# Attention inside a four-layer kernel: other slots for the projection and output products, and rotations of queries that are held back some slots

## The chip, the cores and the metric

The kernel runs on one NeuronCore of a Trainium2 chip. A NeuronCore has several engines that each work through a queue of their own in order: TensorE (PE in the profile) multiplies matrices and transposes, VectorE (DVE), ScalarE (ACT) and GpSimd (POOL) do elementwise work, and SyncE (SP) issues most DMA transfers. Engines wait for each other by semaphores. The metric is the device time of one execution in microseconds (us); the number given for a kernel is the median of its runs.

## The reference

Four pairs of a conditioning layer and a feed-forward layer are added to `x` (64 sequences of 32 tokens, width 512), one after the other. The change lies in the third pair, in attention over a paged cache:

```python
q = einsum('bsd,ed->bse', x, Wq).reshape(b, s, 32, 128)   # Wk, Wv: 8 heads
q = rope(rmsnorm(q, q_norm_w), pos); k = rope(rmsnorm(k, k_norm_w), pos)
k_all = concatenate([k_cache[block_table], k]); v_all = concatenate([v_cache[block_table], v])
scores = where(valid, q @ k_all.T * SCALE, -1e30)         # 512 cached keys + 32 own keys
o = softmax(scores) @ v_all
return einsum('bse,de->bsd', o, Wo)
```

All matrices are float32. What counts below: queries and keys are projected, normalised and rotated before they are used, each sequence attends to 512 cached keys and its own 32, and the heads' outputs go through the output projection `Wo`.

## The kernel before

`emit` runs three stages: `layer0`, `layer1` and `attention`, with the rest (`Tail`) behind attention. Attention takes two thirds of the time, and the change is in it alone.

**Tiles and steps.** The 2048 tokens are 16 tiles of 128 tokens, four sequences in each. The 8 key heads are done in two halves of four. A *step* is one half of the heads with one tile; there are 32 steps. Two steps that follow each other are a *pair*; there are 16 pairs. A step has 16 *turns* (four sequences times four key heads), so a pair has 32 turns and the kernel 512. A turn handles 128 rows: four query heads times 32 tokens.

**A turn on TensorE.** The loop is at L1233. Turn `i` turns the probabilities of its own turn (`turned`, L1000: four transposes into `prT_ps`, copied by ScalarE at L1004), does the extra work of slot `2t`, makes the scores of the turn two ahead (`start(i + 2)`, `scores`, L974), does the extra work of slot `2t + 1`, and multiplies by the values (`values`, L1015, into the accumulators `po`). `scores` is followed on VectorE by an add of the mask that also takes the minimum (L991), on ScalarE by the exponential with its sum (L993), and on VectorE again by a reciprocal (L995) and a multiplication of the probabilities (L998). After each second sequence `own_part` (L1023) adds the sequences' own values and two copies (L1034, one on ScalarE, one on VectorE) empty `po` into `oT`. After each sequence four gathers on GpSimd's queue fetch the next values (L738), and VectorE copies own values into place (L745).

**The extra work.** Between the turns' own instructions the kernel places, by numbers of slots written out by hand, the projections of the pair that follows and the output projection of the pair before. A pair has 64 slots; a number from 64 on is a slot in the next pair. The order of TensorE's instructions is the program's: `on_pe` (L76) chains them. The other engines' queues are ordered by the framework's scheduler when the kernel is built.

Both projections use a scheme with seven products instead of eight for a 2 by 2 block matrix:

- `Projections.product` (L846): seven products `m` for each of three groups `g` of columns (`g = 0`: keys and values; `g = 1, 2`: queries), in the order 1, 2, 5, 6, 3, 7, 4. Each is four matmuls of 512 columns. ScalarE takes the result out for `m` 1 and 5 (L857), VectorE adds it for the others (L865); `m` 3 and 7 have a second add (L867, L870).
- After products 2, 3, 7 and 4 of the queries one block is complete, and its rotation (`rotated`, L768) is put on the list `soon`. The list is emptied at the start of the next slot (`the_rest`, called in `slot`, L1150). A rotation is a square on ScalarE (L761), on VectorE a sum (L763), a scaling (L764), two half-width products (L775) and one of full width (L778), and on GpSimd a power (L130), an add (L779) and a product (L780).
- `Projections.turned` (L874) transposes a rotated block on TensorE (`qkT_ps`), and ScalarE copies it to `qT` (L883), from which scores are made.
- `Outputs.product` (L936): seven products, each in two pieces `u = 0` and `u = 1` of eight matmuls of 256 columns. Both pieces go into one accumulator, taken out after the second (L955 on ScalarE or L959 on VectorE). Between the two pieces the accumulator stays in use.

All these products share the PSUM tag `mm` with two buffers:

```python
acc = ps.tile([P, D], F32, tag="mm", bufs=2, name="pq" if g else "pkv")     # L851
self.acc = ps.tile([P, D], F32, tag="mm", bufs=2, name="py")[:, :H]         # L941
```

Each product is followed by a request for the weights of the product four later (`next_wp`, `next_wo`: one transfer of 512 KB on SyncE's queue into one of four buffers). Requests stand on the list `later`, of which each slot issues up to two, between the parts of the keys' loads.

Of the kernel before, what the change touches and what calls it, by code (L numbers as in the profile page):

```python
# [664 lines left out]
def attention(c, known, x_in, y_part, y_out, sums, tail):  # L665
# [18 lines left out]
    with ExitStack() as outer:  # L684
# [63 lines left out]

        soon = []

        def the_rest():
            for f in soon:
                f()
            del soon[:]
# [286 lines left out]
        per = SEQ * HKP  # L1041
# [34 lines left out]
        outputs = [Outputs(n) for n in range(len(steps) // 2)]  # L1076


        later, to_come = [], {}
        wos, wos_to_come = [], [partial(wo_piece, o.h, m, u) for o in outputs for m in ORDER  # L1080
                                for u in range(2)]

# [67 lines left out]
        def slot(fs):  # L1150
            now = later[:]
            del later[:]
            the_rest()
            for f in now[:2]:
                f()
            later[:] = now[2:]
            for f in fs:
                f()

        for s, (h, T) in enumerate(steps):  # L1160
# [6 lines left out]
            def at(i, *fs):  # L1167
                to_come.setdefault(s * 2 * per + i, []).extend(fs)
# [3 lines left out]
            if s % 2 == 0:  # L1172
# [7 lines left out]
                if not last_pair:  # L1180
                    p = projections[n + 1]
                    if n == 0:
                        ats = ((12, 14, 16, 17, 18, 20, 22), (24, 26, 28, 32, 33, 34, 38),
                               (40, 42, 44, 48, 49, 52, 56))
                        then = ((0, 0, 0, 21), (0, 1, 0, 29))
                        for i, f in zip((3, 5, 6, 7, 10), (partial(p.x, 0), partial(p.x, 1), p.x_sums,
                                                           partial(p.tables, "k"), partial(p.tables, "q"))):
                            at(i, f)
                    else:
                        ats = ((2, 6, 8, 12, 14, 17, 20), (22, 26, 28, 32, 34, 36, 40),  # L1190
                               (42, 44, 46, 49, 50, 54, 58))
                        then = ((0, 0, 0, 13), (0, 1, 0, 27))
                        at(3, partial(p.tables, "q"))
                    for *what, i in (*then, (1, 0, 0, 35), (1, 0, 1, 41), (1, 1, 1, 43), (1, 1, 0, 51),
                                     (2, 0, 0, 53), (2, 0, 1, 57), (2, 1, 1, 67), (2, 1, 0, 69)):
                        at(i, partial(p.turned, *what))
                    for g in range(GB):
                        for m, i in zip(p.ORDER, ats[g]):
                            at(i, partial(p.product, g, m), partial(later.append, next_wp))
                    if n + 2 < len(projections):  # L1200
                        then = projections[n + 2]
                        for i, f in zip((30, 40, 59, 61, 62), (then.load, partial(then.tables, "k"),
                                                               partial(then.x, 0), partial(then.x, 1),
                                                               then.x_sums)):
                            at(i, f)
                else:
                    for i, f in zip((4, 8, 12, 16, 20), tail.weights(xp, wk, op, wp_tile)):
                        at(i, f)
                    at(43, tail.scaled)
                    for m, i in enumerate((45, 48, 49, 61)):  # L1210
                        at(i, partial(tail.fold, ps, m))
                    at(52, outputs[n].first_blocks)
                    for i, where in enumerate((52, 54, 57, 59)):
                        at(where, partial(outputs[n].product, i), partial(later.append, next_wo))
                if n:
                    out = outputs[n - 1]
                    at(0, partial(out.first_sums, nc.gpsimd))
                    if out.h:
                        at(14, out.befores)
                    ats = (0, 1, 5, 9, 13, 16, 17, 21, 25, 29, 32, 33, 37, 41) if last_pair else \  # L1220
                        (0, 1, 4, 10, 16, 18, 24, 30, 33, 38, 48, 52, 56, 60)
                    for i, where in enumerate(ats):
                        at(where, partial(out.product, i), partial(later.append, next_wo))
                        if i in (5, 7):
                            for u in range(2):
                                at(where, partial(out.next_sum, 6 if i == 5 else 3, u))
                    at(47 if last_pair else 63, out.store)
                else:
                    for i in (40, 46, 52, 58):
                        at(i, next_wo)  # L1230
            for at in range(2 * per):
                slots[at].extend(to_come.pop(s * 2 * per + at, []))
            for t in range(per):  # L1233
                i = s * per + t
                _, _, b, g = of(i)
                prT = turned(i)
                if g == HKP - 1:
                    own_prTs = ([] if b % 2 == 0 else own_prTs) + [own_turned(b)]
                slot(slots[2 * t])
                start(i + 2)  # L1240
                if g == 1:

                    keys_of(i - 1 + 2 * HKP)
                slot(slots[2 * t + 1])
                values(b, g, prT)
                if b % 2 and g == HKP - 1:
                    own_part(b, own_prTs, oTs[s])
# [348 lines left out]
```

## Time and profile before

| what | value |
|---|---|
| median of 3 runs | 3628.14 us (3626.78 to 3630.88) |
| the profiled execution's own time | 3624.15 us |
| its span, first to last instruction | 3622.4 us |
| TensorE busy | 3529.3 us, 97% |
| VectorE, GpSimd, ScalarE busy | 2094.9, 1604.6, 1315.1 us |
| mean granted TensorE clock | 0.996 |
| one pair in the middle (1839.6 to 1986.3 us) | 146.7 us |
| DMA in that pair | 0.78 of the engines' time, 248 GB/s |

How to read it: matmuls are pipelined, and their recorded ends are modelled, so the busy share of TensorE says little about small stalls. Four transposes of one group start 0.109 us apart though each is recorded with 0.275 us; four matmuls of 512 columns start 0.429 us apart and are recorded with 0.592 us. A stall is therefore best read from start to start; the idle time that the profile states for it is 0.15 to 0.2 us shorter. "Idle before, releaser" names what ended a wait.

### The profile page before, as it was taken

The numbers are of one execution on the slowest core, as the hardware profiler recorded it, in microseconds if no ns is written. First come the engines' busy times: TensorE is split into PE (matmuls) and PEld (weight loads), VectorE is DVE, ScalarE is ACT, GpSimd is POOL, SyncE is SP. The second block draws the span as 40 slices with busy tenths as digits, with TensorE's granted clock in tenths as the row PEclk, the third lists the DMA queues.
The fourth block names the chain that finished last, engine by engine and source line by source line (L and its number), as shares of the span: only waits on it lengthen the run. The fifth ranks groups of instructions, "written<-read, shape, count | busy, mean of one in ns | idle before, by whom it ended". The sixth has DMA issues, their size and how long they took to land.

```text
span 3622.4 us, 61570 instructions
## 1 busy us (share of the span) xinstructions
PE 3529.3 (97%) x19328; PEld 2629.3 (73%) x19328; DVE 2094.9 (58%) x5268; ACT 1315.1 (36%) x3110; POOL 1604.6 (44%) x1607
## 2 busy tenths in 40 slices
PE   8999999999998999999999999999999999999999
PEld 3444788888866777777777777777777777778755
DVE  5443222222237777767777777777776777767433
ACT  1111111111114544444444444444444544445311
POOL 0112432222226645546456465555565645645232
PEclk9999999999999999999999999999999999999999
DMA  5003543333336777787777777778778778777631
GB/s 210 26 26 136 176 136 117 105 103 103 100 120 207 241 253 242 248 257 242 252 236 248 256 242 246 249 249 257 254 249 262 238 258 254 252 249 247 205 95 62
DMA packets 610341, 716.00 MB, mean 198 GB/s; under 512 B 61826, under 2 KB 469378, under 8 KB 610018
## 3 DMA queue, kind: packets, MB, share of 16 engines
q1 hardware_dynamic: 557538, 539.01, 47.6%
q0 software_dynamic: 50176, 168.86, 13.7%
q10 hardware_dynamic: 2304, 4.20, 0.3%
q8 instruction: 158, 2.59, 0.3%
q14 instruction: 165, 1.35, 0.1%
HBM read 669.88 MB, written 41.94 MB: 197 GB/s over the span
## 4 chain that ended last, share of the span: by engine, by line
PE 87%; DVE 7%; ACT 2%; DMA 2%; issue 2%; POOL 1%; SPq 0%; DVEq 0%; ACTq 0%; POOLq 0%
PE po L712 12%; PE sc L986 11%; PE gate_up L366 11%; PE py L712 10%; PE pq L712 8%; PE prT_ps L707 5%; PE pkv L712 5%; PE pz L366 5%; PE po L1362 3%; PE ph L126 3%; PE pd L251 3%; PE po L366 2%; PE qkT_ps L707 2%; PE py L206 1%; DVE swapped L775 1%
## 5 line engine op out<-in xcount | busy, mean ns | idle before, releaser
L738 POOL DMA_INDIRECT vt<-in_v_rows,v_rows x512 | 507.5, 991 | 436.5 <-PE po L712 315.2
L986 PE MATMUL sc<-kt,qT 128*128 128x288 f32 (+1 forms) x2048 | 556.7, 394 | 13.6 <-DVE low L991 9.0
L993 ACT ACTIVATE pr<-pr,low 128x544 f32<-128x544 f32 x512 | 383.3, 749 | 505.6 <-DVE low L991 397.5
L712 PEld LDWEIGHTS po<-prT,vt 128*128 128x128 f32 x4096 | 520.6, 192 | 50.5 <-ACT prT L1004 23.0
L712 PE MATMUL po<-prT,vt 128*128 128x128 f32 x4096 | 544.6, 276 | 6.9 <-ACT prT L1004 6.7
L986 PEld LDWEIGHTS sc<-kt,qT 128*128 128x128 f32 x2048 | 384.4, 190 | 221.2 <-issue 107.7
L991 DVE CUSTOM_DVE_ANT_0 pr<-sc,mask 128x544 f32<-128x544 f32 x512 | 368.1, 719 | 149.4 <-PE sc L986 111.7
L998 DVE TENSOR_SCALAR pr<-pr,low 128x512 f32<-128x512 f32 x512 | 345.2, 674 | 11.5
L1004 ACT COPY prT<-prT_ps 128x512 f32<-128x512 f32 x512 | 293.4, 573 | 90.3 <-PE prT_ps L707 38.0
L707 PE MATMUL prT_ps<-ident,pr 128*128 128x128 f32 x2048 | 311.7, 275 | 7.1 <-DVE pr L998 6.9
L779 POOL TENSOR_TENSOR projected<-projected,swapped 128x512 f32<-128x512 f32 x160 | 208.4, 1302 | 193.4 <-DVE projected L778 144.4
L712 PE MATMUL pq<-wp,x_sums 128*128 128x512 f32 x512 | 241.6, 595 | 12.9 <-DVE projected L865 12.9
L707 PEld LDWEIGHTS prT_ps<-ident,pr 128*128 128x128 f32 x2048 | 237.2, 142 | 17.8 <-issue 9.3
L712 PE MATMUL py<-wo,oT 128*128 128x256 f32 x1024 | 243.4, 381 | 0.0
L995 DVE RECIPROCAL low<-low 128x1 f32<-128x1 f32 x512 | 82.2, 161 | 252.1 <-ACT pr L993 231.1
L130 POOL TENSOR_TENSOR rs<-rs,minus_half 128x4 f32<-128x4 f32 x160 | 187.1, 1169 | 75.3 <-DVE rs L764 41.9
L712 PEld LDWEIGHTS py<-wo,oT 128*128 128x128 f32 x1024 | 188.8, 191 | 22.6 <-issue 0.3
L996 ACT ACTIVATE own_pr<-pr,low 128x32 f32<-128x32 f32 x512 | 165.0, 322 | 91.3 <-DVE low L995 58.1
L452 DVE TENSOR_TENSOR sg<-sg,gate_up 128x256 f32<-128x256 f32 (+1 forms) x88 | 37.0, 421 | 269.1 <-ACT sg L451 269.1
L712 PE MATMUL py<-wo,o_sum 128*128 128x256 f32 x768 | 182.9, 382 | 2.1 <-DVE o_sum L922 2.1
L761 ACT ACTIVATE squares<-projected 128x512 f32<-128x512 f32 x160 | 101.0, 631 | 226.8 <-DVE projected L865 128.4
L712 PE MATMUL pq<-wp,xT 128*128 128x512 f32 x384 | 182.3, 597 | 0.2 <-issue 0.2
(242 smaller groups left out, 5833.6 us busy)
## 6 DMA issues: line engine op xcount, KB each, us to landing
kt<-in_kT SPq DMA_DIRECT2D x2048, 64.0 KB
wp<-in_sums SPq DMA_DIRECT2D x192, 512.0 KB
wo<-out_sums SPq DMA_DIRECT2D x128, 512.0 KB
wp<-in_WqT SPq DMA_DIRECT2D x96, 512.0 KB
wo<-in_WoT SPq DMA_DIRECT2D x96, 512.0 KB
wp<-in_WkT SPq DMA_DIRECT2D x32, 512.0 KB
xt<-x SPq DMA_DIRECT2D x48, 256.0 KB
in_sums<-sums POOLq DMA_DIRECT2D x24, 512.0 KB, 5.1
```

Of the source, the lines that this page charges most:

```text
L130: self.nc.gpsimd.tensor_tensor(t, t, self.minus_half[:, :n], ALU.pow)
L366: c.on_pe(nc.tensor.matmul(out, lhsT, rhs, start=start, stop=stop))
L707: c.on_pe(nc.tensor.transpose(pt[:, m, :], piece, c.ident))
L712: c.on_pe(nc.tensor.matmul(out, lhsT, rhs, start=first and i == 0, stop=last and i == len(pairs) - 1))
L738: nc.gpsimd.indirect_dma_start(out=vts[b % 2][:, n, :], out_offset=None, in_=a["v_rows"], in_offset=bass.IndirectOffsetOnAxis(ap=rows[h][: ...
L779: nc.gpsimd.tensor_tensor(src, src, tmp, ALU.add)
L986: c.on_pe(nc.tensor.matmul(sc[:, lo + n * PSIZE:lo + m * PSIZE].rearrange("p (n k) -> p n k", k=PSIZE), q, kt[:, n:m, g, :], start=True, s ...
L991: nc.vector.tensor_tensor_reduce(pr[:, :NK], sc[:, lo:lo + NK], masks[h, b], -SCALE, 3.0e38, ALU.add, ALU.min, low[:, 0:1])
L993: nc.scalar.activation(pr[:, :NK], pr[:, :NK], AF.Exp, bias=low[:, 0:1], scale=-1.0, accum_out=low[:, 1:2])
L996: nc.scalar.activation(own_prs[b % 2][:, g * S:(g + 1) * S], pr[:, L:NK], AF.Copy, scale=low[:, 2:3])
L998: nc.vector.tensor_scalar(pr[:, :L], pr[:, :L], low[:, 2:3], None, ALU.mult)
L1004: last_prT.append(nc.scalar.copy(prT, pt).ins)
```

## The change

The products keep their order within their kind, and TensorE, VectorE, ScalarE, GpSimd and the DMA queues issue the same instructions as before. Other things are altered in the pairs after the first:

- Slots of the output product's pieces: 4, 10 become 6, 8; 16, 18 become 16, 17; 24, 30 become 24, 26; 33, 38 become 32, 33; 48, 52 become 48, 49. (0, 1 and 56, 60 stay. The last pair keeps its own list.) Slots 16, 32 and 48 follow the turn that ends with `own_part`.
- Slots of the projections' products, moved so that the number of products in each turn stays the same.
- In all pairs, after products 2, 3, 7 and 4 of the queries `put_off` takes the rotation from `soon` and files it under a slot 2, 0, 2 or 4 slots after the next one. `slot` gets what is filed ahead of its own list.
- In all pairs, slots of the queries' transposes (`turned`) move from 35, 41, 43, 51, 53, 57, 67, 69 to 37, 43, 51, 53, 57, 65, 67, 73.

```diff
+        WAIT = {2: 2, 3: 0, 7: 2, 4: 4}
+        def put_off(i, to):
+            to.setdefault(i, []).extend(soon)
+            del soon[:]
...
-                        ats = ((2, 6, 8, 12, 14, 17, 20), (22, 26, 28, 32, 34, 36, 40),
-                               (42, 44, 46, 49, 50, 54, 58))
+                        ats = ((2, 4, 10, 12, 14, 18, 20), (22, 28, 30, 34, 36, 38, 40),
+                               (42, 44, 46, 50, 52, 54, 58))
...
-                    for *what, i in (*then, (1, 0, 0, 35), (1, 0, 1, 41), (1, 1, 1, 43), (1, 1, 0, 51),
-                                     (2, 0, 0, 53), (2, 0, 1, 57), (2, 1, 1, 67), (2, 1, 0, 69)):
+                    for *what, i in (*then, (1, 0, 0, 37), (1, 0, 1, 43), (1, 1, 1, 51), (1, 1, 0, 53),
+                                     (2, 0, 0, 57), (2, 0, 1, 65), (2, 1, 1, 67), (2, 1, 0, 73)):
                         at(i, partial(p.turned, *what))
                     for g in range(GB):
                         for m, i in zip(p.ORDER, ats[g]):
                             at(i, partial(p.product, g, m), partial(later.append, next_wp))
+                            if g and m != 1 and m != 5 and m != 6:
+                                at(i, partial(put_off, s * 2 * per + i + 1 + WAIT[m], waiting))
...
-                        (0, 1, 4, 10, 16, 18, 24, 30, 33, 38, 48, 52, 56, 60)
+                        (0, 1, 6, 8, 16, 17, 24, 26, 32, 33, 48, 49, 56, 60)
...
-                slot(slots[2 * t])
+                slot(waiting.pop(2 * i, []) + slots[2 * t])
...
-                slot(slots[2 * t + 1])
+                slot(waiting.pop(2 * i + 1, []) + slots[2 * t + 1])
```

## The prediction

> **What bounds the kernel now.** I read the page's head and chain first: TensorE.
>
> ```profile
> span 3622.4 us, 61570 instructions
> PE 3529.3 (97%) x19328; PEld 2629.3 (73%) x19328; DVE 2094.9 (58%) x5268; ACT 1315.1 (36%) x3110; POOL 1604.6 (44%) x1607
> PE 87%; DVE 7%; ACT 2%; DMA 2%; issue 2%; POOL 1%; SPq 0%; DVEq 0%; ACTq 0%; POOLq 0%
> ```
>
> No matmul is removed, so only TensorE's stalls can be won. The view of waits, for TensorE from 1250 to 3290 us (pairs 1 to 14), has in each line what waited, for whom, us in total, times and the longest:
>
> ```profile
> PE pq L712 <- DVE projected L865: 12.9, 12, 1.3
> PE prT_ps L707 <- DVE pr L998: 6.0, 14, 0.4
> PE pkv L712 <- ACT y L955: 3.1, 13, 0.2
> PE sc L986 <- DVE low L991: 2.5, 12, 0.2
> PE po L712 <- ACT prT L1004: 2.1, 13, 0.2
> ```
>
> Five waits, about once a pair each: the same places in every pair. TensorE's timeline of pair 5 gives the places (start, length, and at the end the idle time with its releaser). Turn 3, slot 6:
>
> ```profile
> 1855.24 0.27 PE L707 MATMUL own_prT_ps<-ident,own_pr 128*128 128x128 f32 x1
> 1855.75 1.98 PE L712 MATMUL pkv<-wp,xT 128*128 128x512 f32 x4 [0.24 <-ACT y L955]
> ```
>
> Turns 20, 23 and 25 (slots 40, 46, 50):
>
> ```profile
> 1931.36 0.63 PE L707 MATMUL prT_ps<-ident,pr 128*128 128x128 f32 x4 [0.43 <-DVE pr L998]
> ...
> 1946.80 1.18 PE L986 MATMUL sc<-kt,qT 128*128 128x288 f32 x4 [0.21 <-DVE low L991]
> 1948.14 1.16 PE L712 MATMUL po<-prT,vt 128*128 128x128 f32 x8 [0.16 <-ACT prT L1004]
> ...
> 1956.06 0.60 PE L707 MATMUL prT_ps<-ident,pr 128*128 128x128 f32 x4
> 1957.92 1.98 PE L712 MATMUL pq<-wp,x_sums 128*128 128x512 f32 x4 [1.25 <-DVE projected L865]
> ```
>
> Stalls are larger than the idle time stated. Transposes start 0.109 us apart, so the product after 1956.06 could have begun at 1956.50 and began 1.42 later. Counted like this, start to start against each group's usual step, pairs 1 to 14 lose 53 us: turn 25 16.5, turn 23 11.8, turn 20 8.7, turn 3 6.6, turn 8 1.2, and 8.4 (0.6 a pair) in spots that belong to the turns themselves, mostly own part and what follows it.
>
> **The change part by part.** *Pieces beside each other.* Instructions stay the same; what moves is how long a piece holds one of the two `mm` buffers. Before, pieces at 48 and 52 hold one; products 6 and 3 of the last group at 49 and 50 share the other. The second must wait until VectorE has added the first (L865), which stands in VectorE's queue behind a reciprocal that waits for the exponential: the 1.42 us. After, the pieces stand at 48 and 49 and products at 50, 52, 54 have both buffers. Going through the built order for which buffer each product takes and where its eviction stands, only the products at 2 and 4 still share one in a row, with 2.7 us of TensorE's work between (scores 0.92, transposes 0.44, values 0.90, transposes 0.44) for a copy of 0.59. So turn 25 goes: −16.5. At slot 6 the buffer was that of pieces 0 and 1, whose copy the scheduler had put on ScalarE behind an exponential two turns later; now it stands a turn earlier, and slot 4's product takes the other buffer: −6.6. Turn 8's product at 17, on a shared buffer, goes to 18: −1.2.
>
> *Rotations held back.* A rotation costs VectorE 2.32 us (0.67 + 2 × 0.41 + 0.68 + 0.15); a turn's softmax 1.63 (0.72 + 0.08 + 0.16 + 0.67); an eviction 0.69, two for products 3 and 7; mask 0.49, key copy 0.22. A turn on TensorE is about 4.0 us (0.44 + 0.92 + 0.90 and a product of 1.73), 4.4 with a transposed block. I summed VectorE's queue from the scores for one turn to the next in the built order. Before: 6.05 against TensorE's 4.43 for turn 19, then 4.37 against 4.11: VectorE is late by 1.9, and the probabilities of turn 20 with it. For turn 23: 5.36 against 4.43; the minimum, thus exponential and next scores, come late. After, for turns 19 to 25: 3.72, 5.34, 3.81, 3.29, 4.95, 3.40, 4.31 against 3.99, 4.54, 3.99, 3.99, 4.43, 4.10, 4.55. The worst excess is 0.80, no longer two in a row. Following turn 20's chain: probabilities ready 3.8 us after its scores, transposes reached 5.3 after: 1.5 spare. For turns 21 and 22 1.4 and 1.1 remain. The old order treated alike gives a stall of 0.7 at turn 20 (0.59 is there) and, at turn 23, 0.55 at the values (0.32) and none at the scores (0.37): good to about 0.3. So turns 20 and 23 go: −20.5.
>
> *What it queues up.* The tightest place left is turn 24: values need `po` emptied, and VectorE's copy (L1034, 0.69) comes 0.3 to 0.4 us before TensorE arrives; the two pieces at 48 and 49 (3.46 us) are its cover, and any delay shows one for one. I charge 0.3 us a pair, the method's error: +4. At a pair's end the rotation at 63 puts a sum and a product ahead of that copy (5.67 against 4.55 for turn 1), but `po` is wanted 6.7 us after the scores and free after 4.5. Nothing.
>
> *Later transposes.* From rotation to transposes there are 6 slots or more in both versions, some 13.7 us, for 2.3 on VectorE, 3.5 on GpSimd (1.17 + 1.30 + 1.04) and a set of gathers ahead of it on GpSimd (5.2). The earliest user is slot 65's block: scores at slot 66's end need it, with values, transposes and a product (3.1 us) as cover for a copy of 0.58 that stands before the exponential on ScalarE. Nothing; uncovered it would cost up to 1 us a pair.
>
> *Weights.* SyncE's requests move with the products, among the keys' 64 KB loads. By the order on SyncE and what each must wait for, the shortest lead is 7 slots, before (slot 50) and after (slot 42), about 16 us, but 7, 8 and 8 now follow each other. By the packets' times, 512 KB loads of `in_sums` landed 3.1 to 8.9 us after issue. Hidden, for either sign.
>
> *First pair.* Its products stay; rotations move. It loses 17.6 us to stalls, some 8 of them from turn 18 on. Sums for turn 18 don't change (6.03), for turn 19 they fall (4.87 to 3.36), for turn 23 rise (4.26 to 5.51), for turns 28 and 29 go from 3.96 and 2.73 to 2.04 and 4.24. Between −5 and +5; I take 0.
>
> **A rule against it.** The rows: L998 has 674 ns on average on the page, but
>
> ```profile
> L998 DVE TENSOR_SCALAR pr<-pr,low x446: 470/487/3033, 1250.8 to 3289.3; 128x512 f32<-128x512 f32 x149
> ```
>
> (shortest/median/longest): some 128 of the 446 are over 60 ns longer than the median, mostly beside GpSimd's adds, products and gathers. The Trainium skill, "SBUF — State Buffer", section "Who interferes with whom", explains this: VectorE's copies and `tensor_scalar` in two-port modes and GpSimd share a port pair that one holds for a whole instruction while the other blocks. The change brings rotations to 37, 41, 45, 47. By the rows (0.67 holds the average loss) the sum is as above. By the rule at its harshest each of six turns' L998 waits out a GpSimd operation of about 1.2 us in place of the 0.19 it loses on average: 6.1 us a pair, of which about 1.1 is spare, so 5.0 of new stall against 3.2 won, +25 us over 14 pairs. I take the rows: before, the same four rotations stand in 35 to 45, equally dense.
>
> **Sum.** −16.5 − 6.6 − 1.2 − 20.5 + 4 ± 0 = −40.8, say −40. Span 3622.4 − 40 = 3582.4; the execution's own time was 1.75 above its span (3624.15), the runs' median 4.0 above that: 3588.
>
> **Rivals.**
> - *Half of it comes back* (VectorE waits more between minimum and exponential than the sums show, so stalls move to turns 20 to 26): 20 us or fewer are won, 3605 to 3620. For it: from turn 20 to 25 VectorE's work after the change is 25.1 us against 25.6 of TensorE's. Against: recorded durations overlap on VectorE (a full product of 0.67 is followed after 0.60), so true loads are smaller.
> - *Slower, by the port*: the mechanism above, place turns 20 to 25. It decides from 4.3 us of added blocking a pair (3.2 won, 1.1 spare), 0.7 a turn; at its full price 3653. For it: L764 has 141 to 1269 ns. Against: nothing in GpSimd's amount of work changes, and the old stretch already has these blocks.
> - *No change*: the buffers are not what held TensorE, and another wait ends at the same time. Against: at 1957.92 the releaser is the eviction itself, and there was nothing else to wait for.
>
> **How the numbers follow.** A difference of 0.2% (7 us) is about what can be told from none. Likeliest, 3588 with own range 3577 (all 45 and the first pair won) to 3604: 0.76. Half back: 0.11. No change: 0.03. Slower: 0.10. Range 3577 to 3620 leaves out the last two and little else. Faster 0.87, same 0.03, slower 0.10.
>
> **What would show it.** Right: TensorE's wait for L865 (12.9) and for L955 (3.1) gone, waits for L998 and L991 under 2 us in all from pair 1 to 14, a pair of about 143.8 us in place of 146.7. Wrong: `po` waiting for L1034 at turn 24, `sc` for `qT` at slot 66, a product for `wp` at 42 to 46, or L998's mean well over 674 ns.

## The result

| | before | after |
|---|---|---|
| median of 6 runs each | 3627.46 us (3622.56 to 3632.71) | 3601.36 us (3597.67 to 3603.64) |
| ratio | | 0.9926, 95% interval 0.9916 to 0.9936 |
| span of the profiled execution | 3622.4 us | 3601.9 us |
| mean granted TensorE clock in it | 0.996 | 0.993 |
| typical pair in the middle | 146.7 us | 143.8 us |
| mean of pairs 1 to 14 | 146.4 us | 143.9 us |

The changed kernel is 26 us faster. The forecast was 3588 (3577 to 3620), 40 us faster: the direction and the range held, the size did not.

The changed kernel has seven more lines there, so line numbers behind L748 move by 7: the scores are L993, the minimum L998, the exponential L1000, the scaled probabilities L1005, the copy of `prT` L1011, the copy out of `po` L1041, the evictions L872 and L962, the rotation's sum, scaling, half products and full product L770, L771, L782 and L785, GpSimd's add and product L786 and L787, the first sums L929 and L930.

The page's head and chain:

```profile
span 3601.9 us, 61460 instructions
PE 3526.7 (98%) x19328; PEld 2634.1 (73%) x19328; DVE 2154.5 (60%) x5268; ACT 1301.2 (36%) x3110; POOL 1598.8 (44%) x1607
PE 84%; DVE 8%; DMA 3%; issue 2%; POOL 1%; ACT 1%; SPq 1%; DVEq 0%; another core or an unknown queue 0%; ACTq 0%; POOLq 0%
```

TensorE's waits from 1264.0 to 3277.9 us, which are pairs 1 to 14 here:

```profile
PE prT_ps L707 <- DVE pr L1005: 0.8, 1, 0.8
PE po L712 <- ACT prT L1011: 0.2, 1, 0.2
```

Five waits of 27 us in all have become two of 1 us. The timeline of TensorE shows turns 23 to 25 of a pair in the middle, where 1.42 us were lost before turn 25's product alone:

```profile
1945.08 1.16 PE L712 MATMUL po<-prT,vt 128*128 128x128 f32 x8
1946.17 1.16 PE L712 MATMUL po<-own_prT,own_vt 64*128 64x128 f32 x16
1947.26 0.66 PE L707 MATMUL prT_ps<-ident,pr 128*128 128x128 f32 x4
1947.76 1.89 PE L712 MATMUL py<-wo,o_sum 128*128 128x256 f32 x8
1949.49 1.08 PE L993 MATMUL sc<-kt,qT 128*128 128x288 f32 x4
1950.40 1.46 PE L712 MATMUL py<-wo,o_sum 128*128 128x256 f32 x6
```

The two pieces stand on either side of the scores, and no idle time is recorded (a bracket would stand at a line's end). In the first line, turn 23, something is still lost that the idle column leaves out: the four scores before it begin at 1943.87 and take 0.92, so the values could start at 1944.79 and start 0.29 later.

Stalls counted from start to start, as in the prediction, by turn over pairs 1 to 14 (us; turns 8, 23 and 31 hold 0.8, 1.3 and 1.4 that belong to the turns themselves):

| kernel | turn 3 | 8 | 20 | 21 | 23 | 25 | 31 | others | sum | pairs 1 to 14 last |
|---|---|---|---|---|---|---|---|---|---|---|
| before | 6.6 | 2.0 | 8.7 | 0 | 13.1 | 16.5 | 1.4 | 5.0 | 53.1 | 2049.0 |
| after | 1.2 | 3.5 | 0 | 0 | 6.8 | 0 | 1.6 | 5.3 | 18.4 | 2014.4 |

The sum falls by 34.7 and the 14 pairs by 34.6: the stalls account for all that happened in these pairs. But the span fell by 20.5 only. The rest was given back outside:

| stretch of the profiled execution | before | after | difference |
|---|---|---|---|
| ahead of attention (its code is unchanged) | 1066.0 | 1075.0 | +9.0 |
| first pair | 138.3 | 139.6 | +1.3 |
| pairs 1 to 14 | 2049.0 | 2014.4 | −34.6 |
| last pair | 149.8 | 153.6 | +3.8 |
| loads and products ahead of pair 0, and all behind the last pair | 219.2 | 219.3 | 0.1 |

**Ahead of attention** TensorE waits in the same places as before, a little longer. The two lines of waits up to 1070 us that differ most, after and then before ("issue": it waited for nothing that the profile shows):

```profile
PE pz L366 <- issue: 6.4, 3, 3.3
PE low_ps L366 <- issue: 4.5, 2, 4.1
```

```profile
PE pz L366 <- issue: 4.7, 3, 2.0
...
PE low_ps L366 <- issue: 3.4, 2, 3.0
```

That is 2.8 us. The larger part is what follows such a wait. In a table of windows of TensorE's activity (busy time and instructions of each engine; the third figure from the end is the granted clock), after and before:

```profile
801.00:808.00 7.00, 6.20 (x15) 4.97 (x16) 0.00 (x0) 0.59 (x1) 0.00 (x0) 0.51 0.01 2
889.00:896.00 7.00, 5.07 (x13) 4.00 (x14) 1.29 (x2) 0.59 (x1) 0.00 (x0) 0.56 0.01 2
```

```profile
801.00:808.00 7.00, 7.00 (x36) 6.18 (x35) 0.82 (x2) 0.97 (x2) 0.96 (x1) 0.98 0.17 40
889.00:896.00 7.00, 7.00 (x38) 6.28 (x37) 1.43 (x5) 2.48 (x6) 0.81 (x1) 1.00 0.14 37
```

In the first window a wait of 3.31 us ends at 801.80, and TensorE does 15 matmuls where the kernel before does 36: it works at half its clock (0.51 against 0.98). The stretches at half clock ahead of attention add up to 27.3 us after and 13.7 before; half of the difference, 6.8, with the 2.8 of longer waits makes 9.6, against the 9.0 observed. The Trainium skill, "TensorE: Matmul & The Clock Gate", "Part 1: The HAM clock gate", says that the clock is set by a free-running window of 3413 ns: after about one idle window it is halved, and after one of work it is whole again. The lengths here agree: each measures 3.4, 6.8 or 10.2 us (but for the last, which the end of the execution cuts). If that is so, equal waits can cost differently, by where in a window they fall; the run "rotations only" below has 14 equal waits of which half are followed by half clock.

The time ahead of attention goes with these stretches in all profiles of this case, whichever kernel: 13.7 us at half clock go with 1064.4 to 1067.2 us (both kernels are among these), 17.1 with 1067.1 to 1068.6, 20.5 with 1069.4 and 1070.3, 23.9 with 1071.1 and 1071.7, 27.3 with 1075.0 and 1075.2. So these 9 us belong to the execution, not to the change, as far as the profiles show. (The three profiles of the changed kernel start attention at 1071.1 us on average, those of the kernel before at 1066.3; so few can't tell this from chance.) What lengthens the waits by "issue" stays open.

**The last pair.** VectorE's timeline at its start:

```profile
3280.22 0.69 DVE L1041 COPY oT<-po 128x512 f32<-128x512 f32 x1 [1.05 <-remote]
3280.94 8.62 DVE L745 COPY own_vt<-v 32x128 f32<-32x128 f32 x5
3289.59 0.72 DVE L998 CUSTOM_DVE_ANT_0 pr<-sc,mask 128x544 f32<-128x544 f32 x1
```

and GpSimd's:

```profile
3279.20 0.95 POOL L738 DMA_INDIRECT vt<-in_v_rows,v_rows  x1 [0.30 <-issue]
3280.17 1.04 POOL L130 TENSOR_TENSOR rs<-rs,minus_half 128x4 f32<-128x4 f32 x1
3281.21 1.26 POOL L786 TENSOR_TENSOR projected<-projected,swapped 128x512 f32<-128x512 f32 x1
3282.64 1.05 POOL L738 DMA_INDIRECT vt<-in_v_rows,v_rows  x1 [0.17 <-issue]
3283.72 1.05 POOL L787 TENSOR_TENSOR projected<-projected,rs 128x512 f32<-128x512 f32 x1
3284.72 2.34 POOL L929 TENSOR_TENSOR o_sum<-oT 128x1024 f32<-128x1024 f32 x1
3287.14 2.34 POOL L930 TENSOR_TENSOR oT<-oT 128x1024 f32<-128x1024 f32 x1
```

Five copies of 32 by 128 took 8.62 us; one of them takes 0.22 when nothing is beside it. They end at 3289.56, right behind GpSimd's last sum (3289.48). Behind them on VectorE stands the minimum of turn 1, and TensorE's scores wait for it:

```profile
3284.20 0.60 PE L707 MATMUL prT_ps<-ident,pr 128*128 128x128 f32 x4
3290.47 2.15 PE L993 MATMUL sc<-kt,qT 128*128 128x288 f32 x4 [5.67 <-DVE low L998]
```

5.8 us are lost, and 6.8 us at half clock follow. The experiments come back to this.

### The profile page after: what moved, and what is told of

Read it like the earlier page. It is cut to its first block, busy times and chain, and to the rows that moved or that the text cites. A ratio compares the mean times of both kernels' runs of the same rounds, so it can differ in the third digit from the quotient of the medians.

```text
span 3601.9 us, 61460 instructions
## 1 busy us (share of the span) xinstructions
PE 3526.7 (98%) x19328; PEld 2634.1 (73%) x19328; DVE 2154.5 (60%) x5268; ACT 1301.2 (36%) x3110; POOL 1598.8 (44%) x1607
## 3 DMA queue, kind: packets, MB, share of 16 engines
q0 software_dynamic: 50176, 168.86, 13.4%
## 4 chain that ended last, share of the span: by engine, by line
PE 84%; DVE 8%; DMA 3%; issue 2%; POOL 1%; ACT 1%; SPq 1%; DVEq 0%; another core or an unknown queue 0%; ACTq 0%; POOLq 0%
PE po L712 12%; PE gate_up L366 11%; PE py L712 11%; PE sc L993 10%; PE pq L712 7%; PE prT_ps L707 5%; PE pkv L712 5%; PE pz L366 5%; PE po L1371 3%; PE ph L126 3%; PE pd L251 3%; PE po L366 2%; PE qkT_ps L707 1%; PE py L206 1%; DVE pr L1005 1%
## 5 line engine op out<-in xcount | busy, mean ns | idle before, releaser
L1000 ACT ACTIVATE pr<-pr,low 128x544 f32<-128x544 f32 x512 | 383.3, 749 | 688.1 <-DVE low L998 556.3
L993 PE MATMUL sc<-kt,qT 128*128 128x288 f32 (+1 forms) x2048 | 557.2, 395 | 15.5 <-DVE low L998 12.6
L993 PEld LDWEIGHTS sc<-kt,qT 128*128 128x128 f32 x2048 | 386.2, 191 | 232.2 <-issue 129.3
L998 DVE CUSTOM_DVE_ANT_0 pr<-sc,mask 128x544 f32<-128x544 f32 x512 | 368.4, 719 | 142.9 <-PE sc L993 119.2
L786 POOL TENSOR_TENSOR projected<-projected,swapped 128x512 f32<-128x512 f32 x160 | 208.3, 1302 | 313.5 <-DVE projected L785 284.5
L1005 DVE TENSOR_SCALAR pr<-pr,low 128x512 f32<-128x512 f32 x512 | 318.4, 622 | 12.6
L1011 ACT COPY prT<-prT_ps 128x512 f32<-128x512 f32 x512 | 294.0, 574 | 75.3 <-PE sc L993 30.8
L745 DVE COPY own_vt<-v 32x128 f32<-32x128 f32 x512 | 164.1, 320 | 22.8 <-issue 4.0
```

The lines of the kernel that those rows point to most:

```text
L786: nc.gpsimd.tensor_tensor(src, src, tmp, ALU.add)
L993: c.on_pe(nc.tensor.matmul(sc[:, lo + n * PSIZE:lo + m * PSIZE].rearrange("p (n k) -> p n k", k=PSIZE), q, kt[:, n:m, g, :], start=True, s ...
L998: nc.vector.tensor_tensor_reduce(pr[:, :NK], sc[:, lo:lo + NK], masks[h, b], -SCALE, 3.0e38, ALU.add, ALU.min, low[:, 0:1])
L1000: nc.scalar.activation(pr[:, :NK], pr[:, :NK], AF.Exp, bias=low[:, 0:1], scale=-1.0, accum_out=low[:, 1:2])
L1005: nc.vector.tensor_scalar(pr[:, :L], pr[:, :L], low[:, 2:3], None, ALU.mult)
L1011: last_prT.append(nc.scalar.copy(prT, pt).ins)
```

## The experiments

Times of one group were taken on one chip, each beside runs of the kernel before there. They came in three groups, and in the first the kernel before itself took 3606.26 us (3596.31 to 3611.09, 21 runs), some 23 us less than in the other sessions. No profile of it was taken there, so where these 23 us lie stays open; ratios of that group may be off by up to 0.6% against the others, and its kernels are best compared with each other and by their stalls. The stalls by turn, in pairs 1 to 14, counted as above:

| kernel | turn 3 | 8 | 20 | 21 | 23 | 25 | 31 | others | sum | pairs 1 to 14 last |
|---|---|---|---|---|---|---|---|---|---|---|
| changed (`e0_after`) | 1.1 | 0.8 | 0 | 0 | 6.7 | 0 | 1.6 | 5.2 | 15.4 | 2011.4 |
| slots only | 0 | 0.8 | 0 | 2.9 | 1.3 | 0 | 18.7 | 6.6 | 30.3 | 2026.4 |
| rotations only | 0.9 | 0.8 | 0 | 2.9 | 3.3 | 45.3 | 1.4 | 5.0 | 59.6 | 2055.6 |
| one pair of pieces | 6.6 | 0.8 | 8.6 | 0 | 13.0 | 0 | 18.8 | 5.6 | 53.3 | 2049.4 |
| that and the last rotation | 26.4 | 1.3 | 8.7 | 0 | 13.4 | 0 | 1.6 | 5.6 | 56.9 | 2053.0 |
| hold the last block only | 4.5 | 3.4 | 0 | 3.0 | 1.3 | 13.9 | 1.6 | 6.6 | 34.4 | 2030.5 |
| before again (`b0_before`) | 6.5 | 1.8 | 8.7 | 0 | 12.9 | 17.8 | 1.4 | 5.2 | 54.4 | 2050.3 |
| before again (`b1_before`) | 6.6 | 1.8 | 8.7 | 0 | 13.2 | 18.5 | 1.4 | 5.0 | 55.1 | 2051.0 |
| changed again (`c0_after`) | 1.0 | 3.0 | 0 | 0 | 6.6 | 0 | 1.6 | 5.2 | 17.4 | 2013.5 |

### First group: the two halves of the change

The changed kernel, unedited, as the base:

> The changed kernel again, for comparison on this chip: 26 us faster than before (ratio 0.9926). In its profile pairs 1 to 14 lose 18 us to TensorE's stalls where before they lost 53, and the last pair stalls 5.8 us at its turn 1. If the 9 us that the first profile lost ahead of attention (layers 0 and 1, which the change does not touch) belong to that execution, attention's first product starts near 1066 us again; if they belong to the program, near 1075 us.

Measured: 3587.85 us (3584.07 to 3591.54), ratio 0.9954 (0.9939 to 0.9970). In its profile pairs 1 to 14 take 2011.4 us with stalls of 15.4, attention starts at 1066.5, and the last pair takes 145.9. The five copies at the last pair's start took:

```profile
3267.25 0.69 DVE L1041 COPY oT<-po 128x512 f32<-128x512 f32 x1
3267.98 2.87 DVE L745 COPY own_vt<-v 32x128 f32<-32x128 f32 x5
```

So what happens in pairs 1 to 14 is the program's; what happened ahead of attention and at the last pair's start is not in every execution.

Slots only (the change without the rotations' delay):

```diff
                             at(i, partial(p.product, g, m), partial(later.append, next_wp))
-                            if g and m != 1 and m != 5 and m != 6:
-                                at(i, partial(put_off, s * 2 * per + i + 1 + WAIT[m], waiting))
```

> The changed kernel without holding rotations back: each is issued in the slot after its product again; product slots and transposes as changed. Theory (buffers and rotations are two separate causes): the stalls of turns 25 and 3 go with the slots, 24 us, and those of turns 20 and 23 stay or grow, as rotations now stand at 29, 37, 39, 41; 15 to 24 us faster than before, ratio 0.993 to 0.996. Rival (VectorE's queue is the one cause, and the slots help only through it): under 7 us, ratio above 0.998.

Measured: 3599.22 us, ratio 0.9978 (0.9971 to 0.9986); 11.4 us slower than the changed kernel beside it, and 15.0 in pairs 1 to 14. The row "slots only" answers in a way that the prediction's split doesn't have: the stalls of turns 20 and 23, which I had given to the rotations, are gone with the slots alone (2.9 come up at turn 21), and a new one stands at turn 31. So the expected 15 to 24 us did not come, and of the theory only turns 25 and 3 held. TensorE's timeline there, and VectorE's:

```profile
1973.72 1.18 PE L993 MATMUL sc<-kt,qT 128*128 128x288 f32 x4 [0.54 <-DVE low L998]
1975.07 1.16 PE L712 MATMUL po<-prT,vt 128*128 128x128 f32 x8 [0.16 <-ACT prT L1011]
```

```profile
1966.01 0.69 DVE L872 TENSOR_TENSOR projected<-pq,projected 128x512 f32<-128x512 f32 x1 [0.30 <-PE pq L712]
1966.81 2.24 DVE L782 TENSOR_TENSOR swapped<-projected,q_sin 128x256 f32<-128x256 f32 x1
```

The rotation of the last block goes out at slot 59, straight behind its eviction; the first half product takes 2.24 us in place of 0.41, beside a gather and an add on GpSimd, and VectorE has not made up for it at turn 31.

Rotations only (the old slots, with the delays and the later transposes):

```diff
-                                     (2, 0, 0, 53), (2, 0, 1, 57), (2, 1, 1, 67), (2, 1, 0, 69)):
+                                     (2, 0, 0, 57), (2, 0, 1, 65), (2, 1, 1, 67), (2, 1, 0, 73)):
...
+                            if g and m != 1 and m != 5 and m != 6:
+                                at(i, partial(put_off, s * 2 * per + i + 1 + WAIT[m], waiting))
```

> The changed kernel with the old slots of products: only the rotations are held back and the transposes later. Theory (two separate causes, and the rotation at slot 63 causes the last pair's stall): turns 20 and 23 lose their stalls, 20 us, turn 25 keeps its 1.4 us a pair, and the last pair gains a stall of some 9 us with the clock's half speed after it: 8 to 15 us faster, ratio 0.996 to 0.998. Rival (rotations alone make the gain): 26 us, ratio 0.993.

Measured: 3625.78 us, ratio 1.0057 (1.0041 to 1.0074), 37.9 us slower than the changed kernel beside it, where a gain on the kernel before had been expected. Turns 3, 20 and 23 lose 4.2 us in place of 28.4 (turn 21 gains 2.9), so these stalls go here too; but turn 25, expected to stay, grows from 16.5 to 45.3. The stall expected at the last pair's start did not come: that pair takes 145.9 us. TensorE's waits in that run, turn 25 of one pair on TensorE, what VectorE did in front of the eviction, and what GpSimd did beside it:

```profile
PE pq L712 <- DVE projected L872: 27.8, 13, 2.1
```

```profile
1963.25 1.12 PE L712 MATMUL pq<-wp,x_sums 128*128 128x512 f32 x2 [2.14 <-DVE projected L872]
```

```profile
1959.36 1.41 DVE L745 COPY own_vt<-v 32x128 f32<-32x128 f32 x1
1960.80 0.72 DVE L998 CUSTOM_DVE_ANT_0 pr<-sc,mask 128x544 f32<-128x544 f32 x1
...
1962.44 0.16 DVE L1002 RECIPROCAL low<-low 128x1 f32<-128x1 f32 x1 [0.91 <-ACT pr L1000]
1962.52 0.67 DVE L872 TENSOR_TENSOR projected<-pq,projected 128x512 f32<-128x512 f32 x1
```

```profile
1959.63 1.04 POOL L787 TENSOR_TENSOR projected<-projected,rs 128x512 f32<-128x512 f32 x1
```

One copy of own values took 1.41 us in place of 0.22, and ends at 1960.77, with the product of the delayed rotation on GpSimd (1960.67). In the kernel before no rotation stood there, and the copy took 0.22. The minimum, the exponential, the reciprocal and the eviction behind it come 0.9 to 1.2 us later, and the stall grows from 1.42 to 2.31. In seven of the 14 pairs 3.4 us at half clock follow, though the recorded wait is 2.13 or 2.14 in all 14. Six of these take 147.6 or 147.7 us, where the pairs without take 146.0 (one 146.9): 1.7 more, half of 3.4; the seventh is pair 14, which is shorter in every kernel. The stall of 1.42 before has no half clock behind it in any pair.

Two things are to be read from the two halves together. At turn 3 this run has the old slots 4 and 10 and still no stall: the scheduler has put the copy of `y` (L962, 1860.36 in pair 5) ahead of the exponential (1861.30), behind which it stands in the kernel before. So the place of that copy in ScalarE's queue is the cause, and the new slots are not the only way to move it. And both halves contain the later transposes, while every run with the earlier ones (the kernel before, and two below) keeps the stalls of turns 20 and 23. The transposes that move from slot 35 to 37 put 0.44 us of TensorE's work between the scores for turn 20 and the transposes that wait there; the stall at turn 20 is 0.62 a pair. What the transposes do alone was not tried, so the share of slots, delays and transposes in these two turns stays open.

One pair of pieces (the kernel before, with only the pieces at 48 and 52 put next to each other, and two products out of their way):

```diff
-                               (42, 44, 46, 49, 50, 54, 58))
+                               (42, 44, 46, 50, 52, 54, 58))
...
-                        (0, 1, 4, 10, 16, 18, 24, 30, 33, 38, 48, 52, 56, 60)
+                        (0, 1, 4, 10, 16, 18, 24, 30, 33, 38, 48, 49, 56, 60)
```

> The kernel before with one thing changed: output pieces at 48 and 49 (before 48 and 52), and the last group's products 6, 3 at 50, 52 (before 49, 50). Theory (a held accumulator buffer is what stalls turn 25): the wait of pq for L865 goes, 1.42 us less in each of 13 pairs and 0.1 behind it, 16 us faster in all, ratio 0.9955. Rival (another wait ends at the same time): within 5 us, with a new wait at turns 25 or 26.

Measured: 3621.19 us, ratio 1.0043 (1.0028 to 1.0059). Turn 25's stall is gone whole, 16.5 to 0, as the held buffer says. And nothing is won: pairs 1 to 14 take 2049.4 us, as before, since turn 31 now loses 18.8 in place of 1.4: the same stall as in "slots only", in a kernel with the old slots. (By time it is 15 us slower than the kernel before on that chip; without a profile of that one there, where these lie stays open.) Two readings fit. VectorE used to gain 1.4 us on TensorE while that stood at turn 25, and no longer does; or the two products that moved a turn back put their additions a turn nearer to the last block's rotation. This run changes both and doesn't tell them apart.

### Second group: does holding the last rotation finish the job?

The kernel before, unedited, for a profile beside these:

> The kernel before, profiled where the others of this call are. Theory (its stalls are its own, the same everywhere): attention from its first product to its last near 2386 us, pairs near 146.7 us, and a difference in its total comes from ahead of attention. Rival (its stalls depend on who gets the port that VectorE and GpSimd share, and so on the execution): pairs of another length, 145.5 us or so, and the difference sits in them.

Measured: 3631.15 us, ratio 1.0007 (0.9999 to 1.0015) against the other runs of the same kernel; stalls by turn as in the first profile within 1.3 us.

One pair of pieces, and the last block's rotation held from 59 to 63, with its last transposes at 73 in place of 69 (all else as before):

```diff
+                            if n and g == 2 and m == 4:
+                                at(i, partial(put_off, s * 2 * per + 63, waiting))
```

> The kernel with pieces at 48 and 49 and products at 50, 52, and in addition the rotation of each pair's last block held back from slot 59 to 63 (its transposes from 69 to 73). Theory (the stall that went at turn 25 came back at turn 31, because the rotation at 59 made VectorE late there): turn 31's 1.1 us at the scores and 0.3 at the values go, pairs of about 145.1 us instead of 146.5, some 19 us faster than the version with the pieces alone. Rival (VectorE is late at turn 31 for another reason): pairs stay at 146.5.

Measured: 3639.83 us, ratio 1.0034 (1.0021 to 1.0047). Turn 31's stall is gone (18.8 to 1.6) and turn 3 has it (6.6 to 26.4). TensorE's waits (line numbers move by 5 here):

```profile
PE pkv L712 <- ACT y L960: 12.3, 13, 0.9
PE prT_ps L707 <- DVE pr L1003: 11.9, 20, 1.2
```

The first line is the wait for the output product's copy on ScalarE at slot 6, which the change removes through its slots 6 and 8. On ScalarE that copy stands behind the exponential; the rotation at 63 makes the minimum late, the exponential with it, and so the copy. In two pairs (at 2439.27 and 2735.57) half clock follows two waits that end 1.7 us apart, of 1.18 or 0.94 us and 0.94 us, neither of which reaches 1.25 us alone. The stall has moved from turn 25 to 31 to turn 3, and kept its size: 16.5, 18.8 (17.4 of it new), 26.4 (19.8 new).

The changed kernel with the delay for product 4 alone:

```diff
-                            if g and m != 1 and m != 5 and m != 6:
+                            if g and m == 4:
```

> The changed kernel with the rotation held back after product 4 alone; after products 2, 3, 7 it is issued in the next slot again. Theory (of the holds, that of the last block does the work): pairs near the 143.6 us of the full change, against 144.7 without any hold; within 4 us of the full change. Rival (holds after 2 and 7 are needed for turns 20 to 25): pairs of 144.3 us or more.

Measured: 3611.41 us, ratio 0.9955 (0.9942 to 0.9969). Turn 31 is free, but turn 25 loses 13.9 us, in another form than before: scores and values that wait for VectorE, not a product for a buffer. By the order of the program, the rotation of product 4 of the middle group, held to slot 45, now falls on that of product 2 of the last group, which is due at 45 as well; in the changed kernel the latter waits until 47. So the delays are one schedule and not separate gains; that this meeting makes the 13.9 us is argued from the order, not shown.

The changed kernel with the last pair's first sums on VectorE, to take GpSimd out of that place:

```diff
-                    at(0, partial(out.first_sums, nc.gpsimd))
+                    at(0, partial(out.first_sums, nc.vector if last_pair else nc.gpsimd))
```

> The changed kernel with the two sums at the start of the last pair's output product on VectorE instead of GpSimd (as the end of the kernel has them). Theory (in one execution GpSimd held the shared port through a rotation and these sums, VectorE's copies took 8.62 us and TensorE stood 5.8 us): the last pair takes 145 to 147 us whatever the execution; 0 to 8 us faster than the changed kernel, and less spread. Rival (the stall had another cause): the last pair can take 153 us here too.

Measured: 3592.96 us (3587.05 to 3594.48), ratio 0.9899 (0.9885 to 0.9913). The profile's last pair takes 151.4 us with a stall of 3.0 at its turn 1, so the expected 145 to 147 was missed; the reading that fits is that the sums now cost VectorE time of its own.

### Third group: the last pair

The changed kernel and the kernel before, unedited, on this chip:

> The changed kernel unedited, as the base for the two runs with the early last rotation. Theory (who gets the port is drawn anew by each execution): pairs 1 to 14 take 2011 to 2015 us again, and the last pair either 146 or 150 to 154. Rival (the stall at the last pair's start is fixed by the program): 153 to 154 again. The time against before: ratio 0.990 to 0.996.

> The kernel before, unedited, with a profile on the same chip as the changed kernel. By what the first two profiles show its pairs 1 to 14 take 2049 to 2051 us and its last pair 149 to 151; the ratio is 1.000 within 0.0015. If its time is again near 3606 us, as in the session of the first experiments, the theory (the difference lies ahead of attention) has pairs of 146.4 us and attention starting at 1050 us or earlier; the rival (the pairs themselves are faster there) has pairs of 145.5 us or less.

Measured: changed 3601.38 us (3597.93 to 3602.69), ratio 0.9920 (0.9906 to 0.9933), pairs 1 to 14 in 2013.5 and the last pair in 156.6, above the 150 to 154 expected; before 3633.38, ratio 1.0005 (0.9996 to 1.0014), 2051.0 and 152.2. The low time of the first session did not come again, so the two accounts of it stay untested.

In the changed kernel the five copies took 8.59 us again, with 5.8 lost on TensorE. Across the three profiles of it, what differs is the copy out of `po` in front of them. In pairs 2 to 14 (but for pair 9, where no gather is beside it) it starts 0.02 to 0.03 us ahead of a gather of GpSimd's. In the last pair of `e0_after` both start in the same hundredth (3267.25), the copy does not wait, and of the five own copies four take at most 0.27 us and one 1.86, and all are through before GpSimd's product and sums follow each other. In the other two, VectorE is idle for 1.05 us, which the profile puts down to an unknown releaser and which ends 0.07 us behind the gather; the copies then run into these. That the gather holds the port that the copy wants is argued from these times, not shown. In these three profiles an order of starts that 0.02 us decide goes with a stall of 5.8. A copy out of `po` that is late for another reason has the same behind it: in "hold the last block only" and in "that and the last rotation" it waits for TensorE by the profile, and an own copy of 4.12 or 4.13 us and stalls of 5.8 and 6.1 follow.

The last block's rotation, in the one pair ahead of the last, at slot 59 in place of 63, so that GpSimd's add and product are done before the sums:

```diff
-                                at(i, partial(put_off, s * 2 * per + i + 1 + WAIT[m], waiting))
+                                at(i, partial(put_off, s * 2 * per + i + 1 + (0 if m == 4 and g == 2 and n + 2 == len(projections) else WAIT[m]), waiting))
```

> Edit: in the one pair ahead of the last pair, the rotation after product 4 of the last group goes out at slot 59 (as before the change) in place of 63; all else is as after the change. Theory (GpSimd's adds and products of that held rotation, followed by its sums for the output product, keep VectorE from the port at the start of the last pair; this is what made the last pair 153.6 us in the first profile of the changed kernel): the last pair takes 145 to 148 us, no stall of the scores over 1 us there, and the time is 3 to 8 us below that of the unedited changed kernel on the same chip, if that kernel's last pair is again 150 us or more; where it is 146, no difference. Rival (the sums on GpSimd alone do it): last pair unchanged, at 150 us or more.

Measured: 3593.54 us (3584.73 to 3603.16), ratio 0.9892 (0.9877 to 0.9907). The own copies there (shortest, median, longest in ns), in this kernel and in the unedited one on the same chip:

```profile
L745 DVE COPY own_vt<-v x8: 216/220/334, 3278.2 to 3281.6; 32x128 f32<-32x128 f32 x8
```

```profile
L745 DVE COPY own_vt<-v x8: 207/228/4125, 3274.1 to 3283.1; 32x128 f32<-32x128 f32 x8
```

GpSimd's first sum in this kernel:

```profile
3283.32 2.36 POOL L929 TENSOR_TENSOR o_sum<-oT 128x1024 f32<-128x1024 f32 x1
```

No copy is held any more, and the stall at turn 1 is gone, although the sums are still on GpSimd. But the last copy ends at 3281.8, 1.5 us before the sums begin, so this run does not show what the sums would do to copies that met them. The 14 profiles of this case agree on the rotation's part. With it at 63 and the sums on GpSimd the longest of these copies took 1.85 or 1.86 us in two and 4.12 or 4.13 in four; with the rotation at 59 it took 0.34 at most in seven. With the rotation at 63 and the sums on VectorE (`e5_sums_on_vector`) it took 1.62, so the 4.1 us need both. The last pair of this profile takes 152.3 us all the same, against the 145 to 148 expected: at its turn 14 TensorE waits 3.6 us for a load of keys and 2.2 more by "issue", then works at half clock. The kernel before has the same wait there (3.7), and `e0_after` (3.8). In `after` and `c0_after`, which were held up at turn 1, its longest was 2.0 and 2.5: so a part of the 5.8 us would have been spent at turn 14 anyway.

Both together:

```diff
-                    at(0, partial(out.first_sums, nc.gpsimd))
+                    at(0, partial(out.first_sums, nc.vector if last_pair else nc.gpsimd))
```

(and the edit of the run before.)

> Edit: as the run with the last rotation at slot 59, and the first sums of the last pair's output product on VectorE in place of GpSimd. Theory (both loads on GpSimd share the blame): last pair 145 to 147 us, time 3 to 8 us below the unedited changed kernel on the same chip. Rival (the sums cost VectorE what the port cost it): last pair 150 us or more, no gain over the run with the early rotation alone.

Measured: 3591.34 us (3586.22 to 3597.82), ratio 0.9893 (0.9880 to 0.9907), last pair 149.5 us, pairs 1 to 14 2015.2. No gain over the early rotation alone. Both are 8 to 10 us below the changed kernel on that chip, so the early last rotation is the better version of this change, at a ratio of 0.989 to the kernel before (the sums on VectorE alone, at 0.990 in the second group, can't be told from it); a part of the 8 to 10 is a higher clock over the whole run (mean of the runs 0.995 against 0.994, by estimate some 4 us), to which the half clock that followed the stall belongs.

## Why the prediction was right in direction and too large

- *TensorE's stalls alone can be won.* Right: 34.7 us of stalls less, 34.6 us of time less in the same pairs. The signs named for it came too: the waits for the eviction and for the copy of `y` are gone, and those for VectorE's softmax are 0.8 us in all.
- *Turn 25, −16.5, a held buffer.* Right, and shown alone: with those two pieces next to each other, and two products out of their way, it is 0. What the step lacked is the next place: removed alone, 17.4 us come back at turn 31. This term came out by luck: the delays of the rotations, which I had booked elsewhere, keep the 17.4 from coming back.
- *Turn 3, −6.6.* 1.2 left, mostly one instance, so −5.4. The cause, a copy on ScalarE behind an exponential, was confirmed when it grew to 26.4 in the run that made the exponential late, and when it went to 0.9 in "rotations only", where the copy stands ahead of the exponential with the old slots.
- *Turn 8, −1.2.* Wrong by sign and small: +1.5 in the first profile, −1.2 in `e0_after`.
- *Turns 20 and 23, −20.5, by the rotations' delays.* The size was −15.0: turn 20 gone (−8.7), turn 23 from 13.1 to 6.8 (−6.3). The attribution failed: either half of the change takes away most of the 20.5 (2.9 us are left at turns 20 to 23 with the slots, 4.9 with the rotations, 5.5 with both), so the gain can't be booked to the delays. Both halves have the later transposes, and whether these do it was not tried. The step summed VectorE's queue for the old and the new kernel, and never for a kernel with one part only. What is left at turn 23 is of the same kind as what went. ScalarE's timeline there, and VectorE's, beside the values that start at 1945.08 in place of 1944.79:

```profile
1943.72 0.75 ACT L1000 ACTIVATE pr<-pr,low 128x544 f32<-128x544 f32 x1 [3.82 <-DVE low L998]
...
1944.46 0.56 ACT L1011 COPY prT<-prT_ps 128x512 f32<-128x512 f32 x1
```

```profile
1941.25 0.68 DVE L872 TENSOR_TENSOR projected<-pq,projected 128x512 f32<-128x512 f32 x1
1941.85 0.86 DVE L771 TENSOR_SCALAR rs<-rs 128x4 f32<-128x4 f32 x1
1942.63 0.41 DVE L782 TENSOR_TENSOR swapped<-projected,q_sin 128x256 f32<-128x256 f32 x1
1942.96 0.71 DVE L998 CUSTOM_DVE_ANT_0 pr<-sc,mask 128x544 f32<-128x544 f32 x1
```

  ScalarE stood idle for 3.82 us until the minimum was there; the copy of `prT`, whose transposes were done by 1942.2, is behind the exponential in its queue. The minimum is late by a rotation, of which the scaling of 128 by 4 elements took 0.86 us in place of 0.16, its median before. My sums had 4.95 against 4.43 here, and followed the probabilities, not the copy that is queued behind the next exponential.
- *Turn 24's charge, +4.* Not needed: no value waited for L1041. With it left out the pairs' terms give −44.8 against −34.7; the 5.5 missing at turn 23, 2.7 at turn 8 and 1.2 at turn 3 make most of the 10.1.
- *Later transposes, weights.* Right: no wait for `qT` or `wp` in pairs 1 to 14.
- *First pair, between −5 and +5.* +1.3 in the first profile, and 139.2 to 139.9 against 138.3 to 140.0 over three profiles each: nothing.
- *The pair's end: "Nothing".* This step is where the last pair was missed. It counted VectorE's own queue and TensorE's need for `po`. It left out that the rotation at 63 also puts GpSimd's add and product next to the first sums, and that copies on VectorE were held beside these for up to 4.1 us. In pairs 2 to 14 the copies are through in time, and the first sum begins 8.0 us or more after the pair's first transposes; in the last pair it begins after 6.7, and the copies were held in two profiles of three.
- *The port rule.* I weighed it at turns 20 to 25 and on L998 (now L1005), and took the rows. There the rows held: its mean fell from 674 to 622 ns. The rule of the Trainium skill, "SBUF — State Buffer", "Who interferes with whom", fits what happened elsewhere, on the small copies of L745 that stand ahead of a minimum: 4.1 us for one at the last pair's start, 1.41 in "rotations only". But the rule speaks of one instruction that holds the ports, and here a copy was held for longer: that of 4.1 us (from 3283.03 in the first profile, by the single instructions) spans the rest of a gather, L787 and L929, which follow each other within 0.03 us.
- *Span and median.* Nothing was set aside for executions that differ. Ahead of attention the six profiles of the two kernels run from 1064.4 to 1075.0 us, which is as large as a term of the sum.

The measured −26 is then −34.7 in the pairs, with 9 us (by the medians) to 14 (by the first profiles) given back outside them. By the means over three profiles of each kernel, −37.0 in pairs 1 to 14, +4.7 ahead of attention, +1.2 in the last pair and +0.2 in the first, −31 in all. The miss is one of size: 6 us in the pairs, where turn 23 was booked as gone and kept 5.5, and the rest in stretches that the sum took as fixed.

## What to carry to other kernels

When an engine beside TensorE is nearly as busy, a stall that is taken away in one place can return in full in the next: before its whole length is booked as a gain, look for the next turn in which that engine is late. Parts of a change are not additive: work the sum out with each part alone as well. And where a small copy on VectorE stands ahead of something that TensorE waits for, GpSimd's work in a row beside it can count, as here, like work on VectorE's own queue.

## What the runs showed of the hardware that I had not expected

- A copy of 0.22 us on VectorE took up to 4.1 us, and five took 8.6, beside GpSimd's rotation and sums in a row; with the rotation 4 slots earlier they took 0.22 to 0.33 and were through before the sums began.
- A recorded idle time of 2.14 us on TensorE was followed by 3.4 us at half clock in seven pairs of 14; one of 1.25 us never was, but two waits of 0.94 to 1.18 us within 3 us were, in two pairs of "that and the last rotation". The Trainium skill, "TensorE: Matmul & The Clock Gate", "Part 1: The HAM clock gate", speaks of an idle window of about 3.4 us; here shorter waits were enough, which would fit a window that counts work and not only full idleness, but that was not tried. Some 2 us of waiting can thus cost 1.7 us beyond their length.
- In one session the unchanged kernel ran 21 to 25 us below its time in the three others, at the same granted clock (0.9945 on average, against 0.9945 and 0.9947 in two of these). The cause stays open.
